# A two-layer graph network on one core: source tiles in pairs in layer 1, and where its memory and its small work lie

## The chip, the cores and the metric

The kernel runs on one core of a Trainium2 chip. The metric is the device time of one execution, in microseconds (us). A core has five engines that run side by side, each through its own queue of instructions in order: TensorE (PE; its weight loads are listed as PEld), VectorE (DVE), ScalarE (ACT), GpSimd (POOL) and SyncE (SP), which here only starts transfers. Engines wait for one another through semaphores.

## The reference, cut to what matters

Layer 0 is an attention with a random-walk branch, a normalisation, a residual and a second normalisation. Layer 1 is a graph attention with four heads, again with a residual and a normalisation. N is 2708 nodes, D is 256, H is 4 heads of 64.

```python
# layer 0
x = layernorm(x + layer0(x, adj))          # layer0 ends in layernorm(h) * ln_g + ln_b
# layer 1
Wh  = einsum('nd,hdo->nho', x, W)
s_i = einsum('nho,ho->nh', Wh, a_src); s_j = einsum('nho,ho->nh', Wh, a_dst)
e   = leaky_relu(s_i[:, None, :] + s_j[None, :, :], 0.2)
adj[i, i] = 1
att = softmax(where(adj != 0, e, -inf), axis=1)
x   = layernorm(x + einsum('ijh,jho->iho', att, Wh))
```

The kernel writes the exponential of the leaky ReLU as a product: up to factors that cancel in the softmax, exp(e) is max(r_i, t_j) times a factor s_j of the source. So `r` holds the targets' part, `tj` the sources', and `sb` the factor s_j. `v` is Wh already multiplied by s_j.

## The kernel before, in words

The nodes lie in 22 tiles: 16 of 128 rows and 6 of 110. `rows[t]` is the size of tile t and `off[t]` its first row.

**Layer 0** (`fast_layer0`) runs two steps of attention and walk. Its small stages are Python generators: `finish` adds the terms of a target tile, `norms` does its two layer normalisations, and `sources` makes `v`, `sb`, `tj` and `s_src` for layer 1 and stores `v` in device memory. A loop over slots advances them. For the last four tiles (`LATE`) `norms` and `sources` are left for layer 1. Memory comes from pools that lie one behind the other in the order in which they are opened: `heldp`, `finp`, `rowp`, `w0`, `keep` (with `xm`, `ba`, `rinv`, `qT`, `kT1`), `sortp`, `tpp`, `wk`. When layer 0 ends these are given up and the pools of layer 1 are opened from the same address. An instruction of layer 1 that writes there has to wait for the last user of what lay there before. `ba` is what the last attention (L258) reads, and `tpp` holds its turned weights `eT`.

**Layer 1** (`layer1`) goes over three groups of targets (8, 8 and 6 tiles: 1024, 1024 and 660 columns). Within a group it goes over all 22 source tiles; group 0 takes them in another order, `first`, with the late tiles last. `order` lists the 66 steps. For each step n:

- `mask(n)` loads a block of the transposed adjacency (and in group 0 the tile's `v`) through SP's queue and makes it 0 or 1 on ScalarE: Sign (L1193), then Square (L1198). If the source tile lies in the group, GpSimd sets its diagonal between the two (L1196, L1197).
- `weights(n)` computes four tiles `pt`, one for each head, on VectorE (L1272): the maximum of `r` and `tj`, times the mask. There are two sets of `pt`.
- `values(n)` multiplies them with `v` on TensorE (L1283), two heads side by side on 64 columns each; `denominators(n)` does the same with `sb` (L1293), four heads side by side on 32 columns each. Both add up over the 22 source tiles in six PSUM banks `acc`.

At a group's end `acc` is copied to `val` and `den`, and during the next group `settle` turns one target tile after another, divides, adds the residual, normalises and stores. Each normalisation takes the statistics on VectorE, adds the epsilon and takes the power -1/2 on GpSimd, and applies both on VectorE. The settles of the last group have nothing beside them and form the tail. In the middle of a group, `share` and `spread` bring `r` for the next group. `verdict` sums up whether the fast layer 0 was exact; it runs at once, in group 1.

Inside layer 1 the program order fixes what each of the four computing engines does. SP's queue is not in that list (`engines`), and its transfers are ordered by the planner. The loop before is:

```python
for n, (g, i, j) in enumerate(order):
    mask(n + 2)
    ...                      # late tiles, settles, share and spread
    weights(n + 1)
    values(n, (0, 1)); values(n, (2, 3))
    denominators(n)
```

Of the kernel before, what the change touches and what calls it, by code (L numbers as in the profile page):

```python
# [8 lines left out]
F32 = mybir.dt.float32  # L9
BF16 = mybir.dt.bfloat16  # L10
I32 = mybir.dt.int32
AF = mybir.ActivationFunctionType
# [32 lines left out]
def kernel(  # L45
# [61 lines left out]
    offdiag = const.tile([P, P], F32, name="offdiag")  # L107
    nc.vector.tensor_scalar(offdiag, ident, -1.0, 1.0, op0=ALU.mult, op1=ALU.add)
# [21 lines left out]
    def layernorm(dst, src, m):  # L130
# [6 lines left out]
        nc.gpsimd.tensor_scalar(ve[:m], mv[:m, 1:2], LN_EPS, None, op0=ALU.add)  # L137
        rs = small.tile([P, 1], F32, name="ln_rs")
        nc.gpsimd.tensor_tensor(rs[:m], ve[:m], minus_half[:m], op=ALU.pow)
        nc.vector.tensor_scalar(  # L140
# [3 lines left out]
    def sources(t, pool, room):  # L144
# [23 lines left out]
        nc.sync.dma_start(vd[t][:m], vt[:m])  # L168

    def norms(t, xt):  # L170

        m = rows[t]
        hh = xe[:m, t, 0:D]
        for last in range(2):
            st = small.tile([P, 6], F32, name="ln_st")[:m]
            mv = small.tile([P, 2], F32, name="ln_mv")[:m]
            nc.vector.bn_stats(st, hh)
            nc.vector.bn_aggr(mv, st)
            yield
            ve = small.tile([P, 1], F32, name="ln_ve")[:m]  # L180
            rs = small.tile([P, 1], F32, name="ln_rs")[:m]
            nc.gpsimd.tensor_scalar(ve, mv[:, 1:2], LN_EPS, None, op0=ALU.add)
            nc.gpsimd.tensor_tensor(rs, ve, minus_half[:m], op=ALU.pow)
            yield
            nc.vector.tensor_scalar(
                hh, hh, mv[:, 0:1], rs, op0=ALU.subtract, op1=ALU.mult
            )
            yield
            if not last:
                nc.gpsimd.tensor_mul(hh, hh, g_sb[:m])  # L190
                nc.gpsimd.tensor_add(hh, hh, b_sb[:m])
                nc.gpsimd.tensor_add(hh, hh, xt[:m])
                yield
# [73 lines left out]
    def general_layer0():  # L267
        with ExitStack() as l0:
# [199 lines left out]
            def finish(t, xf2, xa2):  # L468
# [23 lines left out]
                layernorm(hh[:m], hh[:m], m)  # L492
# [3 lines left out]
                layernorm(xt, hh[:m], m)  # L496
# [28 lines left out]
    def fast_layer0(ep, adjp):  # L525
# [3 lines left out]
        heldp, finp, rowp, w0, keep, sortp, tpp, wk = (  # L529
            l0.enter_context(tc.tile_pool(name=name, bufs=bufs))  # L530
            for name, bufs in (
                ("heldp", HELD), ("finp", 2), ("rowp", 2), ("w0", 1), ("keep", 1),
                ("sortp", 1), ("tpp", 3), ("wk", 1),
# [57 lines left out]
        ba = keep.tile([P, NT, D], F32, name="ba")  # L591
        rinv = keep.tile([P, NT], F32, name="rinv")
# [9 lines left out]
        kT = [wk.tile([P, HN], F32, name="junk"), keep.tile([P, HN], F32, name="kT1")]  # L602

# [357 lines left out]
        def finish(t, ac, ca, cb):  # L961
# [11 lines left out]
            nc.gpsimd.tensor_add(xt, xt, held.pop(t)[:m])  # L973
            if t < NT - LATE:
                yield
                yield from norms(t, ca)
                yield from sources(t, rowp, lambda: ps_tr.tile([P, 4, P], F32, name="tr"))
# [129 lines left out]
        def verdict(pt):  # L1107
# [4 lines left out]
            for s, r in enumerate(sorted_):  # L1112
# [6 lines left out]
                if s:  # L1119
                    nc.vector.tensor_tensor(wants, wants, haves, op=ALU.min)  # L1120
# [3 lines left out]
                    )  # L1124

# [6 lines left out]
                    )  # L1132

# [3 lines left out]
                else:  # L1137
# [3 lines left out]
                    )  # L1141
                nc.vector.scalar_tensor_tensor(
# [8 lines left out]
            )  # L1151
            nc.tensor.matmul(pt, total, ones, start=True, stop=True)
            nc.vector.tensor_scalar(
# [12 lines left out]
    def layer1(ep, adjp, r=None, verdict=None):  # L1166
        l1 = ExitStack()

        pp, rp, pj, keep = (
            l1.enter_context(tc.tile_pool(name=name, bufs=bufs))  # L1170
            for name, bufs in (("pp", 2), ("rp", 1), ("pj", 2), ("keep1", 1))
        )
        ps_u = l1.enter_context(tc.tile_pool(name="ps_u", bufs=2, space=PSUM))
# [6 lines left out]
        for t in reversed(first):  # L1180
            v[t] = keep.tile([P, H, FO], F32, name=f"v{t}")
# [4 lines left out]
        def neighbours(g, j):  # L1186
# [6 lines left out]
            nc.scalar.activation(bar, bar, AF.Sign)  # L1193
            if j in spans[g]:
                own = bar[:, off[j] - i0 : off[j + 1] - i0]
                nc.gpsimd.tensor_mul(own, own, offdiag[:k, :k])  # L1196
                nc.gpsimd.tensor_add(own, own, ident[:k, :k])  # L1197
            nc.scalar.activation(bar, bar, AF.Square)  # L1198
            return bar

        def settle(g, t, val, den, u, last):
# [12 lines left out]
            if last:  # L1214
# [3 lines left out]
            else:  # L1218
# [8 lines left out]
            st = small.tile([P, 6], F32, name="ln_st")[:m]  # L1227
            mv = small.tile([P, 2], F32, name="ln_mv")[:m]
            nc.vector.bn_stats(st, flat)
            nc.vector.bn_aggr(mv, st)  # L1230
            ve = small.tile([P, 1], F32, name="ln_ve")[:m]
            rs = small.tile([P, 1], F32, name="ln_rs")[:m]
            nc.gpsimd.tensor_scalar(ve, mv[:, 1:2], LN_EPS, None, op0=ALU.add)
            nc.gpsimd.tensor_tensor(rs, ve, minus_half[:m], op=ALU.pow)
            yield
            o = pp.tile([P, D], F32, name="o")[:m]
            nc.vector.tensor_scalar(
                o, flat, mv[:, 0:1], rs, op0=ALU.subtract, op1=ALU.mult
            )
            nc.sync.dma_start(out[off[t] : off[t + 1], :], o)  # L1240
# [24 lines left out]
        def weights(n):  # L1265
            if n < len(order):
                g, _, j = order[n]
                k, gw = rows[j], off[spans[g][-1] + 1] - off[spans[g][0]]
                probs[n] = [pj.tile([P, GW], F32, name=f"pt{h}") for h in range(H)]
# [30 lines left out]
        def prepared(t):  # L1300

            yield from norms(t, x_late[:, t - NT + LATE, :])
            yield from sources(t, pp, aux)


        late = [prepared(t) for t in range(NT - LATE, NT)] if verdict else []
        rest, running = [], []
        mask(0)
        mask(1)
# [116 lines left out]
```

## Time and profile before

| | |
|---|---|
| median of 3 runs | 1614.43 us (1613.76 to 1616.03) |
| the profiled execution | 1616.12 us, span from first to last instruction 1614.3 us |
| busy: TensorE, VectorE, ScalarE, GpSimd | 1555.1, 1225.7, 758.0, 475.0 us |
| layer 1, group 0 | 1230.6 to 1372.0 us |
| group 1 | 1372.0 to 1502.4 us |
| group 2 | 1502.4 to 1588.6 us |
| tail | 1588.6 to 1604.5 us, then the end of the program |

In the rows of the profile a tile is named without its number, `out<-in` says what is written and read, and the bracket behind a row gives the idle time before it and what ended it. A row of a timeline merges neighbouring instructions of one kind; "x16" is their number. A value or denominator matmul in this number format appears as two records, so one source tile has 16 records of each kind.

### The profile page before, as it was taken

How to read it: one execution, taken by the hardware profiler on the slowest of the kernel's cores; microseconds unless marked ns; L12 is line 12 of the kernel's file. 1: busy time of each engine (PE TensorE's matmuls, PEld its weight loads, DVE VectorE, ACT ScalarE, POOL GpSimd, SP SyncE). 2: the span in 40 equal slices, each digit the busy share in tenths (PEclk: the TensorE clock that was granted, in tenths of full speed). 3: DMA queues.
4: the chain of work that ended last, by engine and by line, in shares of the span. 5: the costliest groups of instructions: out<-in, count | busy, mean ns of one | idle time of the engine just before them, and what ended most of it. 6: DMA issues, size and time to landing. Idle time of an engine off the chain costs nothing.

```text
span 1614.3 us, 23771 instructions
## 1 busy us (share of the span) xinstructions
PE 1555.1 (96%) x8029; PEld 1032.9 (64%) x8029; DVE 1225.7 (76%) x3669; ACT 758.0 (47%) x1324; POOL 475.0 (29%) x908
## 2 busy tenths in 40 slices
PE   6999999999998999999999999999999989998994
PEld 3477777776776888787778888777785322222342
DVE  2777677677309767877878888989885969999995
ACT  2444444444345455555555665556633334443441
POOL 1311000001023122232124554555533820162143
PEclk9999999999999999999999999999999999999997
DMA  7200000000034333333333334343244242342331
GB/s 200 77 13 17 9 9 12 10 9 13 8 92 107 98 86 96 91 76 84 78 97 96 99 104 118 102 110 94 73 115 148 78 150 84 97 139 77 86 95 30
DMA packets 172493, 128.26 MB, mean 79 GB/s; under 512 B 44342, under 2 KB 161804, under 8 KB 172362
## 3 DMA queue, kind: packets, MB, share of 16 engines
q1 hardware_dynamic: 166442, 115.87, 26.5%
q0 software_dynamic: 3648, 9.26, 1.8%
q10 hardware_dynamic: 2272, 1.52, 0.3%
q8 instruction: 65, 1.06, 0.3%
q14 instruction: 66, 0.54, 0.1%
HBM read 111.78 MB, written 13.46 MB: 78 GB/s over the span
## 4 chain that ended last, share of the span: by engine, by line
PE 83%; DVE 9%; DMA 3%; POOL 2%; ACT 1%; issue 1%; SPq 0%; ACTq 0%; POOLq 0%; DVEq 0%
PE att L258 25%; PE walk L893 24%; PE acc L1283 8%; PE lg L658 7%; PE tr L240 6%; DVE pt L1272 5%; PE acc L1293 4%; PE tr L938 2%; PE tr L952 2%; DMA blk<-in_adjT_dram 2%; PE tr L155 1%; PE lg L628 1%; PE tr L628 1%; DMA xa<-in_w1T_dram 0%; POOL blk L1197 0%
## 5 line engine op out<-in xcount | busy, mean ns | idle before, releaser
L245 ACT COPY eT<-tr 128x512 f32<-128x512 f32 (+5 forms) x264 | 141.5, 537 | 289.2 <-PE tr L240 286.4
L683 ACT ACTIVATE junk<-e,minus,rth 128x2708 bf16<-128x2708 f32 (+1 forms) x88 | 232.8, 2646 | 19.5 <-POOL rth L715 18.6
L1283 PE MATMUL acc<-pt,v 128*64 128x512 f32 (+3 forms) x1056 | 227.9, 560 | 5.9 <-DVE pt L1272 3.7
L258 PE MATMUL att<-ba,eT 128*128 128x256 f32 (+3 forms) x968 | 230.8, 379 | 0.7 <-ACT eT L245 0.7
L258 PE MATMUL att<-xm,eT 128*128 128x256 f32 (+3 forms) x968 | 230.9, 380 | 0.4 <-ACT xa L1021 0.4
L893 PE MATMUL walk<-xe,blk 128*128 128x257 f32 (+3 forms) x968 | 225.3, 384 | 5.0 <-DVE xf L907 5.0
L893 PE MATMUL walk<-xm,blk 128*128 128x256 f32 (+3 forms) x968 | 222.1, 380 | 1.2 <-DVE xw L966 1.2
L893 PEld LDWEIGHTS walk<-xe,blk 128*128 128x128 f32 (+3 forms) x968 | 178.4, 186 | 50.3 <-issue 12.2
L1272 DVE SCALAR_TENSOR_TENSOR pt<-e,tj,blk 128x1024 f32<-128x1024 f32 (+3 forms) x176 | 190.1, 1142 | 25.0 <-PE att L258 9.4
L893 PEld LDWEIGHTS walk<-xm,blk 128*128 128x128 f32 (+3 forms) x968 | 177.6, 186 | 35.4 <-issue 4.2
L258 PEld LDWEIGHTS att<-ba,eT 128*128 128x128 f32 (+3 forms) x968 | 169.5, 186 | 22.4 <-ACT eT L245 1.2
L258 PEld LDWEIGHTS att<-xm,eT 128*128 128x128 f32 (+3 forms) x968 | 169.5, 186 | 22.1 <-ACT xa L1021 0.8
L662 ACT ACTIVATE e<-lg 128x1024 f32<-128x1024 f32 (+1 forms) x132 | 121.1, 922 | 115.0 <-PE lg L658 111.4
L1283 PEld LDWEIGHTS acc<-pt,v 128*64 128x64 f32 (+1 forms) x1056 | 74.4, 138 | 146.2 <-issue 108.2
L763 DVE MAX8 cand<-e 128x8 f32<-128x170 f32 (+1 forms) x352 | 89.6, 322 | 90.7 <-ACT e L662 90.6
L240 PEld LDWEIGHTS tr<-ident,e 128*128 128x128 f32 (+3 forms) x968 | 115.2, 138 | 55.7 <-issue 21.0
L240 PE MATMUL tr<-ident,e 128*128 128x128 f32 (+3 forms) x968 | 147.0, 271 | 0.3 <-ACT xe L944 0.3
L1193 ACT ACTIVATE blk<-blk 128x1024 f32<-128x1024 f32 (+3 forms) x66 | 63.2, 957 | 161.4 <-DMA blk<-in_adjT_dram 148.4
L1293 PE MATMUL acc<-pt,sb 128*32 128x512 f32 (+3 forms) x1056 | 113.6, 548 | 0.0
L1272 DVE SCALAR_TENSOR_TENSOR pt<-r,tj,blk 128x1024 f32<-128x1024 f32 (+1 forms) x88 | 111.1, 1324 | 3.2 <-PE acc L1293 2.1
L763 DVE MAX8 cand<-scr 128x8 f32<-128x97 f32 (+1 forms) x616 | 102.0, 244 | 0.0
L907 DVE TENSOR_TENSOR xf<-walk,xe 128x257 f32<-128x257 f32 (+1 forms) x22 | 9.4, 426 | 110.8 <-PE walk L893 110.8
(215 smaller groups left out, 1987.5 us busy)
## 6 DMA issues: line engine op xcount, KB each, us to landing
blk<-in_adjT_dram SPq DMA_DIRECT2D x32, 704.0 KB
blk<-in_adjT_dram SPq DMA_DIRECT2D x32, 512.0 KB
blk<-in_adjT_dram SPq DMA_DIRECT2D x48, 330.0 KB
blk<-in_adjT_dram SPq DMA_DIRECT2D x32, 320.0 KB
blk<-in_adjT_dram SPq DMA_DIRECT2D x12, 605.0 KB
blk<-in_adjT_dram SPq DMA_DIRECT2D x12, 440.0 KB
blk<-in_adjT_dram SPq DMA_DIRECT2D x18, 283.6 KB
c<-cs POOLq DMA_DIRECT2D x32, 128.0 KB, 2.0
```

The source lines that it names most:

```text
L240: nc.tensor.transpose(tr[: rows[t], q, :m], e[:m, off[t] : off[t + 1]], ident[:m, :m])
L245: copy(eT[:k, : len(grp), :m], tr[:k, : len(grp), :m])
L258: nc.tensor.matmul(acc, eT[: rows[t], q, :m], value(t), start=(t == 0), stop=(t == NT - 1),)
L658: nc.tensor.matmul(lg[:m, h, :w], qT[part, cols], kT[s][part, c0 : c0 + w], start=True, stop=True,)
L662: nc.scalar.activation(halves[:m, :, c0 : c0 + w], lg[:m, :, :w], AF.Exp, accum_out=zp[:m, n : n + 1],)
L683: nc.scalar.activation(junk[:m], e[:m], func, scale=rth, bias=minus1[:m], accum_out=acc)
L763: nc.vector.max(cand[:, n, :], src[:m, n * size : min(N, (n + 1) * size)])
L893: nc.tensor.matmul(ac[:m, :w], blk[: rows[j], j - j0, :m], cur[: rows[j], j, 0:w], start=(j == 0), stop=(j == NT - 1),)
L1193: nc.scalar.activation(bar, bar, AF.Sign)
L1272: nc.vector.scalar_tensor_tensor(pt[:k, :gw], targets[g][h // 2][:k, h % 2, :gw], tj[:k, j, h : h + 1], bar, op0=ALU.max, op1=ALU.mult,)
L1283: nc.tensor.matmul(acc[h // 2][c][q * FO : (q + 1) * FO, :w], v[j][:k, h, :], probs[n][h][:k, c0 : c0 + w], **at,)
L1293: nc.tensor.matmul(acc[2][c][h * 32 : (h + 1) * 32, :w], sb[:k, j, h : h + 1].to_broadcast([k, 32]), probs[n][h][:k, c0 : c0 + w], **at,)
```

## The change

1. **Pairs.** The loop of layer 1 goes over two source tiles at a time: the values of both, then the denominators of both. What stood at the head of each step is now the function `beside`, called before the first and after the denominators; only the first two of the late generators advance in a call.
2. **Other space.** There are three sets of `pt` (12 tiles, `DEEP = 3`) in place of two. Masks and weights are issued further ahead: three masks and two sets of weights before the loop. The pools of both layers are opened in another order: `ba` has a pool of its own behind `tpp` and `sortp`, and in layer 1 `pt` follows `pp` directly, then `v`, then `rp`. `v` lies in the order in which it is used. `val` and `den` have one buffer in place of two.
3. **Diagonals.** One maximum with the identity on VectorE, after Sign and Square, takes the place of two GpSimd operations between them. `offdiag` is gone.
4. **Norms.** All normalisations use `layernorm`, now a generator. The epsilon is added on VectorE, so GpSimd has one operation, the power. `b_sb` is added to `ca` in `finish` and no longer in `norms`.
5. **Queues and the rest.** The late tiles' `v` and the `out` of all groups but the last are stored from ScalarE's queue. `verdict` is a generator among the late ones. In the tail, even tiles are divided on ScalarE.

The diff, cut:

```diff
@@ layernorm, sources, norms @@
-        nc.gpsimd.tensor_scalar(ve[:m], mv[:m, 1:2], LN_EPS, None, op0=ALU.add)
+        nc.vector.tensor_scalar(ve[:m], mv[:m, 1:2], LN_EPS, None, op0=ALU.add)
         rs = small.tile([P, 1], F32, name="ln_rs")
         nc.gpsimd.tensor_tensor(rs[:m], ve[:m], minus_half[:m], op=ALU.pow)
+        yield
         nc.vector.tensor_scalar(
             dst, src, mv[:m, 0:1], rs[:m], op0=ALU.subtract, op1=ALU.mult
         )
-    def sources(t, pool, room):
+    def sources(t, pool, room, queue=nc.sync):
...
-        nc.sync.dma_start(vd[t][:m], vt[:m])
+        queue.dma_start(vd[t][:m], vt[:m])
...
+        yield from layernorm(hh, hh, m)
+        nc.gpsimd.tensor_mul(hh, hh, g_sb[:m])
+        nc.gpsimd.tensor_add(hh, hh, xt[:m])
+        yield
+        yield from layernorm(hh, hh, m)
+        yield
@@ fast_layer0 @@
-        heldp, finp, rowp, w0, keep, sortp, tpp, wk = (
+        heldp, finp, rowp, w0, keep, tpp, sortp, keepb, wk = (
...
-        ba = keep.tile([P, NT, D], F32, name="ba")
+        ba = keepb.tile([P, NT, D], F32, name="ba")
...
             nc.gpsimd.tensor_add(xt, xt, held.pop(t)[:m])
+            nc.gpsimd.tensor_add(ca[:m], ca[:m], b_sb[:m])
@@ layer1 @@
-            for name, bufs in (("pp", 2), ("rp", 1), ("pj", 2), ("keep1", 1))
+            for name, bufs in (("pp", 2), ("pj", 1), ("keep1", 1), ("rp", 1))
         )
+        DEEP = 3
...
-        for t in reversed(first):
+        for t in first:
             v[t] = keep.tile([P, H, FO], F32, name=f"v{t}")
...
             nc.scalar.activation(bar, bar, AF.Sign)
+            nc.scalar.activation(bar, bar, AF.Square)
             if j in spans[g]:
                 own = bar[:, off[j] - i0 : off[j + 1] - i0]
-                nc.gpsimd.tensor_mul(own, own, offdiag[:k, :k])
-                nc.gpsimd.tensor_add(own, own, ident[:k, :k])
-            nc.scalar.activation(bar, bar, AF.Square)
+                nc.vector.tensor_tensor(own, own, ident[:k, :k], op=ALU.max)
...
-            if last:
+            if last and t % 2:
...
+            yield from layernorm(o, flat, m)
+            if last:
+                nc.sync.dma_start(out[off[t] : off[t + 1], :], o)
+                return
+            yield
+            nc.scalar.dma_start(out[off[t] : off[t + 1], :], o)
...
-                probs[n] = [pj.tile([P, GW], F32, name=f"pt{h}") for h in range(H)]
+                probs[n] = [pj.tile([P, GW], F32, name=f"pt{h}_{n % DEEP}") for h in range(H)]
...
+        if verdict:
+            late.append(verdict(aux))
+        def beside(g, i):
+            for part in late[:2]:
...
+        for n in range(DEEP):
+            mask(n)
+        for n in range(DEEP - 1):
+            weights(n)
+
+        for n in range(0, len(order), 2):
+            g, i, j = order[n]
+            beside(g, i)
+            weights(n + 2)
+            mask(n + 3)
...
+            for u in (n, n + 1):
+                for k in range(2):
+                    values(u, (2 * k, 2 * k + 1))
...
+            for u in (n, n + 1):
+                denominators(u)
...
+            else:
+                beside(g, i + 1)
+            weights(n + 3)
+            mask(n + 4)
```

## The prediction

> **What bounds the kernel now.** I read the page's busy table first, then the table by stretches for the three target groups of layer 1, then TensorE's and VectorE's timelines inside them, the waits, and last the chain at both ends of the layer. The edits outside layer 1 are small, so layer 1 (1230.6 to 1604.5 us) is the place.
>
> ```profile
> 1230.60:1372.00 141.40, 133.67 (x729) 38.94 (x729) 124.15 (x117) 51.58 (x80) 58.53 (x45) 0.98 0.38 117
> 1372.00:1502.40 130.40, 125.95 (x735) 35.58 (x731) 122.53 (x146) 53.57 (x81) 41.65 (x40) 0.97 0.36 102
> 1502.40:1588.60 86.20, 86.20 (x733) 36.09 (x729) 82.64 (x119) 37.47 (x75) 30.33 (x36) 1.00 0.30 82
> ```
>
> Columns: stretch, length, busy time of TensorE, its weight loads, VectorE, ScalarE and GpSimd, clock, DMA. Groups 0, 1 and 2 take 141.4, 130.4 and 86.2 us. TensorE looks fuller, but VectorE is busy for 124, 123 and 83 of them: two engines near their limits.
>
> ```profile
> 1339.38 3.65 PE L1283 MATMUL acc<-pt,v 128*64 128x512 f32 x16
> 1342.96 1.92 PE L1293 MATMUL acc<-pt,sb 128*32 128x512 f32 x16
> 1344.82 3.65 PE L1283 MATMUL acc<-pt,v 128*64 128x512 f32 x16
> ...
> 1502.43 2.44 PE L1283 MATMUL acc<-pt,v 128*64 128x512 f32 x16
> 1504.80 1.32 PE L1293 MATMUL acc<-pt,sb 128*32 128x512 f32 x16
> 1506.05 2.44 PE L1283 MATMUL acc<-pt,v 128*64 128x512 f32 x16
> ```
>
> Undisturbed, a source tile costs TensorE 5.44 us (3.58 values, 1.86 denominators), in group 2 3.62. The single records start 0.429 us apart in the values and 0.430 in the denominators: 8 x 0.429 = 3.43 and 4 x 0.430 = 1.72. The remaining 0.15 + 0.14 = 0.29 us is lost at the two changes of kind; in group 2 it is the same 0.29.
>
> ```profile
> 1222.48 0.72 POOL L972 TENSOR_TENSOR xe<-xe,xw 110x256 f32<-110x256 f32 x1 [5.72 <-ACT xw L968]
> 1230.60 4.47 SPq L1260 DMA_DIRECT2D v<-v  x10
> 1230.62 5.33 DVE L1272 SCALAR_TENSOR_TENSOR pt<-e,tj,blk 128x1024 f32<-128x1024 f32 x4 [9.41 <-PE att L258]
> 1232.78 6.18 PE L1283 MATMUL acc<-pt,v 128*64 128x512 f32 x16 [2.25 <-DMA v<-v]
> ```
>
> The head: VectorE stands 9.4 us until the last attention frees the memory under `pt`; then TensorE waits for the first weights and `v`, and its first values take 6.18 instead of 3.65.
>
> ```profile
> 1241.74 4.85 DVE L1272 SCALAR_TENSOR_TENSOR pt<-e,tj,blk 128x1024 f32<-128x1024 f32 x4
> 1247.39 5.68 DVE L1272 SCALAR_TENSOR_TENSOR pt<-e,tj,blk 128x1024 f32<-128x1024 f32 x4
> 1247.71 1.50 POOL L191 TENSOR_TENSOR xe<-xe,b_sb 110x256 f32<-110x256 f32 x1
> ...
> 1329.52 6.67 DVE L1272 SCALAR_TENSOR_TENSOR pt<-e,tj,blk 128x1024 f32<-128x1024 f32 x5 [6.74 <-ACT blk L1198]
> ...
> 1478.42 0.19 PE L1152 MATMUL aux<-ones,total 128*1 128x1 f32 x2 [4.45 <-DVE total L1149]
> ...
> ACT blk L1198 <- POOL blk L1197: 43.3, 22, 6.2
> ```
>
> VectorE needs 4.79 us for four weights (starts 1.196 apart; the row adds the last one's drain), 5.6 with GpSimd beside it. Its one long stall, 6.74, follows the broadcast of `r`, which delays the mask loads. The verdict stops TensorE for 4.45. The diagonals hold ScalarE 22 times, 43 us, mostly in its slack.
>
> **The change part by part.**
>
> *Pairs.* Two tiles share one change to denominators and one back: 0.29 / 2 = 0.143 us less per tile: 5.294 and 3.474. TensorE's own work: group 0, 22 x 5.294 + 6 for the late sources (four times 1.14 + 0.35) = 122.5; group 1, 116.5 + 8 settles x 0.48 + 0.4 = 120.7; group 2, 76.4 + 3.8 = 80.2.
>
> *Other space, three `pt` sets.* By the sizes in the code, the first two sets of `pt` now lie over `rowp`, `w0` and `xm`. The last users of those are L966, L968 and L972, which ends at 1223.2. So VectorE can start 7.4 us earlier and prepare almost two tiles; the first two `v` lie over `kT1`, long free, so TensorE starts at 1230.6. The other `v` still wait for the attention. If the loads of masks stand behind them on SP, up to 5 us (the row of ten `v`) is lost: rival two. If they don't, nothing; I take nothing.
>
> *Diagonals on VectorE.* Two GpSimd operations leave the path between Sign and Square, 22 VectorE maxima of 128x128 come. No row has that form: below, a 128x22 operation took 0.18; above, 128x154 took 0.315. I take 0.25: 2, 2 and 1.4 us in the groups. A gain here is excluded on VectorE[...]. They now stand in VectorE's queue behind the weights of the tile before and wait there for ScalarE's Square; the next weights and GpSimd's norms are behind them. A load took 4.9 us (1235.98 to 1240.86) and two passes 2.1; two tiles of weights give 9.6. The cover is 2.6 us.
>
> *Norms.* The epsilon addition moves to VectorE: 0.19 each (small dependent operations start 0.15 to 0.19 apart). 8 late norms and 16 settles before the tail, so 1.5 us per group. In layer 0, 36 x 0.19 = 6.8 us more VectorE lie under a TensorE that is 100% busy from 1000 to 1180 while VectorE has 156 of 180; I take 0, and 2 if the search becomes late. `b_sb` moves within GpSimd, sum 0. A norm is then 0.55 (statistics) + 0.19 + 0.33 = 1.07, a settle 1.2 with its reciprocal.
>
> *Queues.* 4 stores of `v` and 16 of `out` go from SP to ScalarE's queue: 20 issues x 0.35 = 7 us, on an engine with 52 of 141 busy. Each waits for its producer, with Sign and Square behind it; the added yield puts the producer half a pair earlier, so 0. SP loses the stops before L168.
>
> *One `val` and `den` instead of two.* The copies at a group's end now wait for the transposes of the group before. Those ended at 1463 and 1564, the copies came at 1500 and 1586: 0. They stand in VectorE's queue between two tiles' weights and wait for the pair's denominators; a copy took 0.7, and I count 0.8 for the waiting in each of two groups. `offdiag` was one operation at the start: 0.
>
> *Verdict.* Its 28 operations, 5 us, go to group 0's second half, and TensorE no longer waits: 4.45 + 2.1 (values of 5.79 instead of 3.65) leave group 1.
>
> [...] The rows: in 1339.3 to 1366.6 TensorE keeps 5.44 per tile and VectorE idles 0.56 before each tile. [...] By the rows TensorE sets these tiles now[...]. I count both loads.
>
> GpSimd's L190 to L192 beside the weights cost VectorE 0.4 per operation (weights 1.58 apart instead of 1.196). [...] 24 remain (8 late, 16 settles): 9.6 by the row[...]. I use the row.
>
> **The sum.** VectorE in group 0, first six pairs: 57.5 weights + 8.6 norms + 3.2 GpSimd + 0.5 + 1.5 waits for GpSimd (a row of 1.5) = 71.3, so 1223.2 to 1294.5. Last five: 47.9 + 1.5 + 5 + the stall of 6.7 = 61.1: 1355.6. TensorE trails by its last value half and the pair's denominators, 1.7 + 3.6: 1361 (its own work of 122.5 from 1230.6 would end at 1353). Before, 1372.0: gain 11. Group 1: eight pairs with settles 9.57 + 1.2 + 0.4 + 0.2 = 11.35 (TensorE 11.07), three at TensorE's 10.59, 1.9 for copies and share: 124.5 instead of 130.4, gain 5.9. Group 2: a pair with settle took VectorE 7.80, now 7.97: 8 x 8.0 + 3 x 6.95 = 85.0 instead of 86.2, gain 1.2. Tail: six chained norms of 2.27, 0.1 less each, one slower ScalarE result: 0.3. Together 18.4. The profiled execution took 1616.1 (span 1614.3, 1.8 around it): 1597.7. It lies 1.7 above the median of the runs, so the forecast is **1596.0**.
>
> **The rivals.** *TensorE stays the bound:* VectorE's stalls vanish too, and 122.5 + 120.7 + 80.2 from 1230.6 ends at 1554, 34.6 earlier: 1579.5. For it: less GpSimd. Against: group 2's VectorE is 96% busy. 0.10.
>
> *The head gains nothing:* `pt` still waits for the attention (7.4 lost, 1603.4), or also the masks behind `v` (4 more, 1607.4). For it: SP's ten `v` in one block at 1230.60. This is also the case that the other space doesn't do what it should. 0.20.
>
> *Slower:* the diagonals make VectorE wait for ScalarE as ScalarE now waits for GpSimd. Each of 22 then costs d more; it decides at d = (18.4 + 3.2) / 22 = 0.98. With 1.2, 26.4 - 18.4: 1622. For it: loads after the broadcast took 7.6. Against: the cover of 2.6. 0.05.
>
> **How the numbers follow.** My case has 0.65 and its own range 1588 to 1604 (loads 4, diagonals 2[...], stalls 6 the other way). 1586 to 1609 takes in most of the second rival and leaves out the first, the slower one and some edge. 0.2% (3.2 us) is about what can be told from no change. Faster 0.93; same 0.03, from the edges of rivals two and three; slower 0.04.
>
> **What would show it.** Right: the first weights near 1223, 32 value records then 32 denominators, about 10.6 us per quiet pair; VectorE over 95% in groups 1 and 2, and TensorE waiting for `pt`. Wrong: a first weight near 1230, a VectorE wait on L1193/L1198 at each diagonal, group 2 clearly under 83 or over 88 us, or a layer 0 that ends elsewhere.

## The result and the profile after

The changed kernel takes 1599.5 us (median of 4 runs, 1598.88 to 1600.24) and the kernel before 1614.22 (4 runs beside it, 1613.76 to 1616.03). The ratio is 0.9906, with a 95% interval of 0.9894 to 0.9918, so the gain is 14.7 us where 18.4 were forecast. The profiled execution of after took 1599.23 us, with a span of 1597.4.

The page's busy table, and the table by stretches for the three groups of layer 1 (length, then TensorE, its weight loads, VectorE, ScalarE, GpSimd, clock, DMA):

```profile
PE 1542.9 (97%) x8029; PEld 1039.1 (65%) x8029; DVE 1226.0 (77%) x3753; ACT 760.4 (48%) x1336; POOL 393.0 (25%) x798
...
1236.17:1364.01 127.84, 125.72 (x732) 39.82 (x732) 117.92 (x148) 50.65 (x79) 17.67 (x17) 0.99 0.43 125
1364.01:1485.08 121.07, 121.07 (x734) 38.09 (x730) 119.30 (x139) 53.11 (x81) 22.62 (x16) 1.00 0.39 108
1485.08:1571.78 86.70, 86.70 (x733) 38.91 (x729) 82.88 (x133) 37.33 (x75) 17.29 (x16) 1.00 0.30 81
```

GpSimd does 82 us less over the whole program. In group 1 TensorE is busy for all of its 121.07 us (before 125.95 of 130.40). VectorE is busy for 98.5% of group 1 and 96% of group 2.

The head of layer 1, in the timeline of after:

```profile
1226.65 10.12 DVE L1258 SCALAR_TENSOR_TENSOR pt<-e,tj,blk 128x1024 f32<-128x1024 f32 x8 [1.72 <-POOL xe L957]
...
1233.59 2.22 SPq L1246 DMA_DIRECT2D v<-v  x5
...
1236.17 7.09 PE L1269 MATMUL acc<-pt,v 128*64 128x512 f32 x32 [2.66 <-DMA v<-v]
...
1243.19 3.64 PE L1279 MATMUL acc<-pt,sb 128*32 128x512 f32 x32
1246.76 7.09 PE L1269 MATMUL acc<-pt,v 128*64 128x512 f32 x32
```

VectorE no longer waits for the attention but for GpSimd's addition at L957, and eight weights come without a stop, 6.9 us before the attention ends. The matmuls come 32 and 32: 10.59 us for a quiet pair (1236.17 to 1246.76). But every `v` was still loaded after the attention (1233.59), and TensorE waited 2.66 us for it.

Laid against one another by the records' times (the end of the last L243/L258, the first value of each group, the last denominator, the last instruction):

| stretch, us | before | after | difference | forecast |
|---|---|---|---|---|
| to the end of the last attention | 1230.53 | 1233.51 | +3.0 | 0 |
| from there to group 1's first value | 141.48 | 130.50 | -11.0 | -11 |
| group 1 | 130.42 | 121.07 | -9.3 | -5.9 |
| group 2, to its last denominators | 86.23 | 86.77 | +0.5 | -1.2 |
| tail | 25.55 | 25.54 | 0.0 | -0.3 |
| sum | 1614.2 | 1597.4 | -16.8 | -18.4 |

The sum is that of the profiled executions. Before's lay 1.9 above its median and after's 0.3 below, hence 14.7 between the medians. The forecast came close partly by luck, by way of a loss and a gain that it did not have: layer 0 became longer, and group 1 shorter than thought. The -11.0 of group 0 is in part luck too (see the first point on why the prediction was right).

**Where layer 0 lost 3 us.** The timeline of after around a late source tile, in layer 0:

```profile
1177.78 3.03 DVE L817 SCALAR_TENSOR_TENSOR e<-scr,fact,e 110x2708 f32<-110x2708 f32 x1
...
1177.94 3.27 POOL L137 TENSOR_TENSOR ln_rs<-ln_ve,minus_half 110x1 f32<-110x1 f32 x1 [6.71 <-DVE ln_ve L135]
...
1183.43 3.47 DVE L733 SCALAR_TENSOR_TENSOR scr<-e,hi 110x2708 f32<-110x2708 f32 x1
...
1187.61 0.41 DVE L139 TENSOR_SCALAR xe<-xe,ln_mv,ln_rs 110x256 f32<-110x256 f32 x1
...
1188.16 0.38 PE L148 MATMUL tr<-ident,xe 110*128 110x110 f32 x2 [2.61 <-DVE xe L139]
```

The last step of a normalisation (L139) stands in VectorE's queue behind the search's large operations, and TensorE, which has the turning of that row (L148) next in its queue, stands for 2.61 us. In before TensorE has no stop above 0.6 us between 913 us and the end of the attention. It is not the epsilon's addition that does this: with it back on GpSimd (experiment 4) the stand is the same,

```profile
1187.38 0.38 PE L148 MATMUL tr<-ident,xe 110*128 110x110 f32 x2 [2.49 <-DVE xe L139]
```

What is left of the change there is the order: before, a normalisation stopped between statistics, power and application; now statistics, epsilon and power come in one turn, so that L139 falls elsewhere among the search's operations. Laid side by side matmul by matmul, after is 2.0 us behind before ahead of this stand, 3.7 behind it, and 3.0 at the attention's end. Experiment 6, which has no such stand, is 2.0 behind at the same place and 0.5 at the end. Where the first 2.0 come from stays open.

**Half-speed windows.** A second thing that the forecast lacked shows in the clock column. TensorE had stretches of 3.41 us in which its clock read 0.50. After, around 1295.6, then before, around 1233.7, by stretches:

```profile
1292.20:1295.60 3.40, 1.82 (x14) 0.60 (x8) 3.40 (x6) 2.35 (x4) 0.00 (x0) 1.00 0.23 29
1295.60:1299.01 3.41, 3.41 (x10) 0.98 (x8) 3.41 (x4) 1.56 (x2) 0.00 (x0) 0.50 0.32 127
1299.01:1302.40 3.39, 3.39 (x18) 1.15 (x16) 3.29 (x5) 0.56 (x1) 0.00 (x0) 1.00 0.51 153
```

```profile
1233.71:1237.12 3.41, 3.41 (x11) 1.12 (x12) 3.38 (x5) 0.00 (x0) 0.52 (x1) 0.50 0.77 225
1237.12:1240.53 3.41, 3.41 (x24) 0.80 (x20) 3.41 (x4) 0.00 (x0) 2.10 (x2) 1.00 0.92 290
```

The waits ahead of the window in after, and what it does to the next 32 values (7.09 us elsewhere):

```profile
1294.51 0.71 PE L148 MATMUL aux<-ident,xe 110*128 110x110 f32 x4 [1.58 <-DVE xe L139]
1295.15 8.78 PE L1269 MATMUL acc<-pt,v 128*64 128x512 f32 x32
```

A window cost 1.7 us where TensorE had work throughout: these values took 8.78 instead of 7.09, 1.69 more, and in experiment 6 8.74, 1.65 more. Before had four of them in layer 1 (1233.7, 1332.7 and two on end at 1476.1), after has one; the tail, where TensorE has little to do, is left out (20.8 us at half clock there in before, 20.6 in after). TensorE stood for part of the pair at 1476.1 (4.45 us, up to 1478.42), and the sixteen values behind that took 5.79 instead of 3.65, so by an estimate from these lengths the windows lost 1.7 + 1.7 + 2.2 = 5.6 us before and 1.7 after. Up to about 3.9 of the 16.8 us are therefore windows that did not come. Of the sixteen values that took 6.18 us, a window makes 1.7 of the 2.5 us above the usual 3.65, and the 5.79 us, which the prediction counted with a wait, are such a window.

Layer 0 had windows as well. Of the eight kernels in which TensorE stands at L148, six (experiments 1, 2, 3, 4, 5 and 7) have one right behind that stand, at 1187.2 to 1189.4; after and experiment 12 have none. In experiment 1:

```profile
1187.89 0.38 PE L148 MATMUL tr<-ident,xe 110*128 110x110 f32 x2 [2.60 <-DVE xe L139]
...
1189.43:1192.84 3.41, 3.41 (x12) 2.57 (x11) 2.10 (x13) 0.79 (x2) 0.00 (x0) 0.50 0.73 160
```

Against before, TensorE falls back by 1.7 us there in after and in experiment 12, and by 3.2 to 3.6 in these six. All kernels but experiments 3 and 7 also have one near 517. In the comparisons below the number of windows is given where it matters; it is known for the profiled executions alone, while the medians come from all.

### The profile page after: what moved, and what is told of

Same layout as the page of the kernel before. It is cut to its first block, busy times and chain, and to the rows that moved or that the text cites. A ratio compares the mean times of both kernels' runs of the same rounds, so it can differ in the third digit from the quotient of the medians.

```text
span 1597.4 us, 23674 instructions
## 1 busy us (share of the span) xinstructions
PE 1542.9 (97%) x8029; PEld 1039.1 (65%) x8029; DVE 1226.0 (77%) x3753; ACT 760.4 (48%) x1336; POOL 393.0 (25%) x798
## 4 chain that ended last, share of the span: by engine, by line
PE 90%; DVE 6%; ACT 1%; issue 1%; POOL 1%; DMA 1%; ACTq 0%; POOLq 0%; DVEq 0%; SPq 0%
PE att L243 25%; PE walk L878 24%; PE acc L1269 13%; PE lg L643 7%; PE tr L225 6%; PE acc L1279 6%; PE tr L923 2%; PE tr L937 2%; DVE pt L1258 1%; PE tr L154 1%; PE lg L613 1%; DVE scr L814 1%; DVE scr L733 1%; PE tr L613 1%; DVE e L817 1%
## 5 line engine op out<-in xcount | busy, mean ns | idle before, releaser
L243 PE MATMUL att<-xm,eT 128*128 128x256 f32 (+3 forms) x968 | 230.9, 380 | 0.4 <-ACT xa L1007 0.4
L243 PE MATMUL att<-ba,eT 128*128 128x256 f32 (+3 forms) x968 | 230.7, 379 | 0.2 <-ACT eT L230 0.2
L1269 PE MATMUL acc<-pt,v 128*64 128x512 f32 (+3 forms) x1056 | 218.0, 549 | 2.9 <-DMA v<-v 2.7
L1258 DVE SCALAR_TENSOR_TENSOR pt<-e,tj,blk 128x1024 f32<-128x1024 f32 (+3 forms) x176 | 186.2, 1122 | 6.2 <-PE acc L1279 2.5
L243 PEld LDWEIGHTS att<-xm,eT 128*128 128x128 f32 (+3 forms) x968 | 169.6, 186 | 22.1 <-ACT xa L1007 0.8
L243 PEld LDWEIGHTS att<-ba,eT 128*128 128x128 f32 (+3 forms) x968 | 169.5, 186 | 21.7 <-ACT eT L230 0.5
L137 POOL TENSOR_TENSOR ln_rs<-ln_ve,minus_half 128x1 f32<-128x1 f32 (+1 forms) x66 | 66.3, 1004 | 224.7 <-DVE ln_ve L135 174.6
L1279 PE MATMUL acc<-pt,sb 128*32 128x512 f32 (+3 forms) x1056 | 106.8, 545 | 0.0
```

Source lines behind the costliest of these rows:

```text
L243: nc.tensor.matmul(acc, eT[: rows[t], q, :m], value(t), start=(t == 0), stop=(t == NT - 1),)
L1258: nc.vector.scalar_tensor_tensor(pt[:k, :gw], targets[g][h // 2][:k, h % 2, :gw], tj[:k, j, h : h + 1], bar, op0=ALU.max, op1=ALU.mult,)
L1269: nc.tensor.matmul(acc[h // 2][c][q * FO : (q + 1) * FO, :w], v[j][:k, h, :], probs[n][h][:k, c0 : c0 + w], **at,)
L1279: nc.tensor.matmul(acc[2][c][h * 32 : (h + 1) * 32, :w], sb[:k, j, h : h + 1].to_broadcast([k, 32]), probs[n][h][:k, c0 : c0 + w], **at,)
```

## The experiments

The first four are the kernel after with one thing undone or moved, the next three remove one cost each, 8 to 11 combine these, and 12 varies the first. Times are medians, each with its ratio to the kernel before that was measured beside it; "after" without more is 1599.5. Those medians of before lie between 1613.96 and 1615.50, so a difference of 1 us between medians of two experiments shows little, and the parts are read from the stages. Stage lengths are from the profiles, by the same records as above.

**1. The pairs alone undone.**

```diff
             for u in (n, n + 1):
                 for k in range(2):
                     values(u, (2 * k, 2 * k + 1))
...
-            for u in (n, n + 1):
-                denominators(u)
+                denominators(u)
```

> The changed kernel, but each tile's denominators follow its own values again (values, denominators, values, denominators); all else stays. The changed kernel took 1599.5. Theory A (TensorE sets groups 0 and 1, VectorE sets group 2): each tile costs TensorE 0.143 us more, so 22 x 0.143 = 3.1 more in group 1, 2 to 3 in group 0, 0 to 1 in group 2: 1604 to 1606. Rival B (VectorE is the bound in all groups after the change): the pairing is covered, 1599 to 1600.5, and group 1 stays at 121.

Measured 1603.39 (0.9924, 0.9908 to 0.9941), 3.9 more than after and a little under theory A's range. By stretches, groups 1 and 2, then TensorE's timeline of one pair with a settle, here and in after:

```profile
1368.37:1491.87 123.50, 123.50 (x734) 34.97 (x730) 119.38 (x139) 53.21 (x81) 22.60 (x16) 1.00 0.38 104
1491.87:1577.43 85.56, 85.56 (x732) 36.30 (x728) 82.94 (x133) 37.20 (x75) 17.27 (x16) 1.00 0.31 81
```

```profile
1391.08 3.65 PE L1269 MATMUL acc<-pt,v 128*64 128x512 f32 x16
1394.66 1.92 PE L1279 MATMUL acc<-pt,sb 128*32 128x512 f32 x16
1396.51 3.65 PE L1269 MATMUL acc<-pt,v 128*64 128x512 f32 x16
...
1402.43 3.65 PE L1269 MATMUL acc<-pt,v 128*64 128x512 f32 x16
```

```profile
1386.65 7.09 PE L1269 MATMUL acc<-pt,v 128*64 128x512 f32 x32
1393.66 3.64 PE L1279 MATMUL acc<-pt,sb 128*32 128x512 f32 x32
...
1397.71 7.09 PE L1269 MATMUL acc<-pt,v 128*64 128x512 f32 x32
```

Group 1 is 2.4 us longer than in after: a pair with a settle takes TensorE 11.35 instead of 11.07, a quiet one 10.88 instead of 10.59, the 0.28 of the forecast, and 11 times that is 3.1. About 0.7 of it is given back: 0.5 at the group's start, where the paired kernel's first pair takes 11.57 while the copies of the group before are made, and 0.2 in its last two pairs. Group 0, from TensorE's start, is 3.0 longer, of which one more window makes 1.7, and layer 0 is 1.8 longer, which its window explains. Group 2, which VectorE sets, is 1.1 *shorter* without pairs: behind the last weights come, in pairs, the denominators of two tiles (a row of 2.43 us) and not of one. With the windows taken off, pairing is worth about 2.5 us in all, less than the 3.9 between the medians.

**2. The early start alone undone:** `ba` goes back into the pool `keep`, so the memory under `pt` is again held by the last attention.

```diff
-            ba = keepb.tile([P, NT, D], F32, name="ba")
+            ba = keep.tile([P, NT, D], F32, name="ba")
```

> The changed kernel, but `ba` lies in the pool `keep` again, so that the pool of `pt` lies over memory that the last attention still reads. Both theories: the first weights start at about 1233.6 instead of 1226.6. Theory A (the early start counts): TensorE's first pair waits for the second tile's weights and group 0 has less lead: 3 to 5 us, 1602.5 to 1604.5. Rival B (TensorE waits for the first `v` until 1236.2 anyway, and group 0 has slack): below 1 us, 1599.5 to 1600.5.

Measured 1608.92 (0.9960, 0.9946 to 0.9974), 9.4 more than after and well above both expectations. VectorE's timeline:

```profile
1234.45 10.59 DVE L1258 SCALAR_TENSOR_TENSOR pt<-e,tj,blk 128x1024 f32<-128x1024 f32 x8 [8.67 <-PE att L243]
```

The first weight comes 7.8 us later than in after and group 1 starts 10.0 later (0.8 of it from a longer layer 0, which has a window; group 0 has one window in both); groups 1 and 2 are the same to 0.01 us. TensorE began within 0.4 us of after, so it is VectorE's start that sets the end of group 0, and almost all of the delay stays. This is the largest single part of the gain.

**3. No diagonals** (the maximum at L1191 is left out, and so are the ones on the diagonal of the mask).

> The changed kernel without the 22 maxima on the diagonal; the diagonals are left as the adjacency has them. It measures what the diagonals on VectorE cost on the path. Theory A (TensorE sets groups 0 and 1): only group 2 gains, six of 0.2: 1 to 1.5 us, 1598 to 1598.5. Rival B (VectorE sets all groups): 22 x 0.2 = 4.4 us, 1595. Rival C (the maxima make VectorE wait for ScalarE's Square): more than 5 us, with the waits on L1188 gone.

Measured 1596.62 (0.9881, 0.9864 to 0.9897), 2.9 less; the profile has one window fewer than after in the whole program, which is 1.7. Group 0 is 1.4 shorter, less than the window of after that this kernel does not have, so nothing is shown there; group 1 0.2, group 2 1.07 for 6 diagonals. The row takes 0.28 us, and the next instruction starts 0.20 after it began (forecast 0.25). In after, VectorE's waits at L1191 are two, nearly all in one of them, where ScalarE had stood for TensorE's projection of a late source tile (L154) with the mask's passes behind it:

```profile
DVE blk L1191 <- ACT blk L1188: 3.5, 2, 3.3
...
1308.61 0.17 ACT L158 ACTIVATE sb<-aux 110x4 f32<-110x4 f32 x1 [9.04 <-PE aux L154]
...
1313.95 0.29 DVE L1191 TENSOR_TENSOR blk<-blk,ident 128x128 f32<-128x128 f32 x1 [3.28 <-ACT blk L1188]
```

That is 3.5 us in all, or 0.16 for each of 22 diagonals, where the third rival needed 0.98; and without the diagonals VectorE still stops for 2.60 us at this point, for the same passes. No run puts the diagonals back on GpSimd, so what moving them gained is not shown, only what they cost on VectorE.

**4. The epsilon on GpSimd again, in all norms.**

```diff
-        nc.vector.tensor_scalar(ve[:m], mv[:m, 1:2], LN_EPS, None, op0=ALU.add)
+        nc.gpsimd.tensor_scalar(ve[:m], mv[:m, 1:2], LN_EPS, None, op0=ALU.add)
```

> The changed kernel with the epsilon of every normalisation added on GpSimd again, two dependent GpSimd operations as before. Theory A (VectorE sets group 2): VectorE is relieved of 8 x 0.15 there, about 1 us gained, 1598 to 1599. Rival D (GpSimd's second small operation is blocked behind the weights, so the results come late and VectorE or TensorE waits for them): 1601 or more, with waits on the power in groups 0 to 2. The 2.6 us that TensorE waits in layer 0 for a normalised row may change with either.

Measured 1594.91 (0.9874, 0.9858 to 0.9891), 4.6 less, a larger gain than theory A's: this part of the change cost time. Group 2 is 1.7 shorter (85.07), which is 8 times 0.21; group 1 0.2; group 0 1.2, no more than the missing window; that window stands in layer 0 instead, which is 0.9 longer, so the two profiles have equally many. The tail is 1.6 shorter, though its last `o` comes 0.8 *later* after the denominators (16.4 against 15.6): between the last `o` and the end of the program lie 7.6 us instead of 10.0. All four kernels with the epsilon on GpSimd have this shorter tail (23.9 to 24.0 us), and its cause stays open, all the more since before, with the same norm, has 9.7 behind the last `o`. Rival D did not come: the two GpSimd operations took 1.18 and 1.46 us beside the weights in before (1241.91 and 1243.17) and 0.22 and 0.57 in the tail here, and no stage of layer 1 became longer by it.

**5. The first two `v` in a pool of their own**, ahead of the others.

```diff
-            v[t] = keep.tile([P, H, FO], F32, name=f"v{t}")
+            v[t] = (early if t in first[:2] else keep).tile([P, H, FO], F32, name=f"v{t}")
```

> The changed kernel, but the first two `v` have a pool of their own between `pt` and the other `v`, at the same addresses. Theory E (an instruction waits for everything that lay under its whole pool, so one pool for all `v` made the first ones wait for the last attention): these two loads start near 1226 instead of 1233.6, TensorE's wait of 2.66 us goes: 1597 (1596.5 to 1597.5). Rival F (the order of SP's queue held them, or TensorE then waits for the second or third weights instead): below 0.7 us, 1599 to 1599.8.

Measured 1600.07 (0.9913, 0.9896 to 0.9930): no gain, and the windows are as many as in after (here in layer 0). The timeline, SP's queue and TensorE:

```profile
1227.63 0.80 SPq L1246 DMA_DIRECT2D v<-v  x2
...
1236.36 7.09 PE L1269 MATMUL acc<-pt,v 128*64 128x512 f32 x32 [0.56 <-ACT xa L1007]
```

Two loads now start 6.0 us before those of after and 8.2 before the attention ends, and TensorE's wait falls from 2.66 to 0.56. So the memory of the first two `v` was free, as the prediction had it, but they were allotted from a pool whose other tiles lay over the attention's memory, and the wait was for the pool. From VectorE's first weight to group 1 it took 135.8 us, as in after without its window (137.4 less 1.7). TensorE's start was not what counted.

**6. One more turn for other work before the normalised source rows** in layer 0, so that VectorE finishes L139 before TensorE comes to L148.

```diff
                 yield from norms(t, ca)
+                yield
```

> The changed kernel with one more yield in layer 0 between the second normalisation and the turning of the row on TensorE. Theory G (the 2.6 us that layer 0 lost are TensorE standing at L148 behind a normalised row that VectorE's search holds back): the wait goes, the last attention ends 2.6 us earlier: 1597 (1596.5 to 1597.5). Rival H (the additional VectorE work of 6.8 us makes the search itself late): the attention ends as now, 1599 to 1600.

Measured 1598.74 (0.9904, 0.9888 to 0.9921). TensorE's timeline:

```profile
1189.68 0.35 PE L148 MATMUL tr<-ident,xe 110*128 110x110 f32 x2
...
1233.19 8.74 PE L1270 MATMUL acc<-pt,v 128*64 128x512 f32 x32 [2.13 <-DMA v<-v]
```

The wait is gone, and the attention ends at 1231.06 instead of 1233.51. Yet the time is within 0.8 us of after: a window more than in after fell on the first values (8.74 instead of 7.09, 1.65 us). From the attention's end group 0 is 1.9 longer, so that 0.3 is left without a cause that I found. Alone this run shows the mechanism and not its worth; runs 8, 9 and 11 do that.

**7. The settles' normalisation applied by ScalarE** (in groups 0 and 1, so during groups 1 and 2). A small GpSimd operation forms the bias.

```diff
+                nc.gpsimd.tensor_scalar(
+                    mr[:m], mv[:m, 0:1], rs[:m], -1.0, op0=ALU.mult, op1=ALU.mult
+                )
...
+                nc.scalar.activation(o, flat, AF.Identity, scale=rs[:m], bias=mr[:m])
```

> The changed kernel, but in the settles before the tail the normalisation is applied on ScalarE, with the product of mean and root made by one more small GpSimd operation. VectorE loses 16 operations of 0.32. Theory A (VectorE sets group 2, TensorE the others): 8 x 0.32 = 2.6 less in group 2, nothing in group 1: 1597 (1596.5 to 1598). Rival B (VectorE sets all groups): 5 us, 1594.5. Rival I (the result now waits on ScalarE behind the masks): 0 or slower.

Measured 1597.46 (0.9894, 0.9877 to 0.9910), 2.0 less. By stretches, groups 1 and 2:

```profile
1365.31:1486.15 120.84, 120.84 (x734) 37.50 (x730) 115.67 (x131) 57.69 (x89) 41.48 (x24) 1.00 0.39 109
1486.15:1570.45 84.30, 84.30 (x733) 38.45 (x729) 80.15 (x125) 41.88 (x83) 29.68 (x24) 1.00 0.31 82
```

VectorE has 3.6 us less to do in group 1, and group 1 does not move (120.84); it has 2.7 less in group 2, and that becomes 2.4 us shorter. So TensorE sets group 1 and VectorE group 2.

**8. Edits 5, 6 and 7 together.**

> The three last edits together: the first two `v` in their own pool, the later turn in layer 0, the normalisation applied on ScalarE. If they are independent, 2.6 + 2.6 + 2.5 less than 1599.5: 1592. If one takes the cover of another (for instance an earlier start that group 0's VectorE can't use), 1594 to 1596.

Measured 1591.90 (0.9865, 0.9849 to 0.9882), 7.6 less than after: alone they gave -0.6, 0.8 and 2.0, which sums to 2.2. Windows make a part of the other 5.4: by the profiles 6 has one more than after, 5 and 7 as many, and this kernel one fewer. At 1.7 each that leaves about 2 without a cause shown. Its profile is 8.5 shorter than that of after: 2.3 in layer 0 (the attention ends at 1231.18), 3.1 in group 0 (TensorE starts at 1231.75; 1.7 is the window), 0.2 in group 1, 2.4 in group 2 and 0.4 in the tail. VectorE's first weight to group 1 takes 134.3 us (135.7 in after without its window).

**9. As 8, and the epsilon on GpSimd.**

> The three edits tried together before (the first two v in a pool of their own, one more turn for other work before the normalised source rows of a target tile, the settles' normalisation applied by ScalarE; 1591.9 us) and the epsilon addition of every norm on GpSimd instead of VectorE. Theory: a 0.2 us VectorE operation per settle costs time where VectorE sets the end, and only there. Group 0 (126.85) and group 2 (84.36) then get shorter by about 1 us each (8 x 0.19 is the ceiling of each, 1.5), group 1 stays at TensorE's 120.8, and the time is 1588.5 to 1590.5. Rival: with the application gone to ScalarE, VectorE no longer sets the end and GpSimd's chain of two small operations per norm does; then nothing is gained, 1591.5 to 1593.

Measured 1587.60 (0.9829, 0.9812 to 0.9845), the fastest kernel here, 11.9 below after and 27.5 below the before measured beside it. By stretches, groups 1 and 2:

```profile
1358.46:1479.30 120.84, 120.84 (x734) 37.46 (x730) 114.11 (x123) 57.72 (x89) 42.76 (x32) 1.00 0.38 109
1479.30:1562.34 83.04, 83.04 (x733) 37.66 (x729) 79.08 (x117) 41.77 (x83) 33.42 (x32) 1.00 0.31 84
```

Group 2 is 1.3 shorter than in 8 and group 1 the same, as expected; group 0 is 0.5 longer and not 1 shorter, counted from a start 0.6 earlier. The tail gives 1.2, as in 4, and brings the time below the 1588.5 to 1590.5 expected.

**10. As 9, with group 2 unpaired.**

> As the kernel with all four edits, but in group 2 the denominators of each tile follow its own values (no pairs there). Theory: group 2 is set by VectorE, and with single tiles TensorE starts its next work half a pair earlier after each pair of weights, which in the unpaired kernel made this group 1.1 us shorter (85.64 against 86.77); here the same 0.5 to 1.1 us less in group 2, groups 0 and 1 unchanged. Rival: VectorE has been relieved so far that TensorE's own work counts; then 11 more changes of kind at 0.29 us make group 2 up to 3 us longer (83.3 is TensorE's own unpaired work, 80.2 paired).

Measured 1588.91 (0.9838, 0.9822 to 0.9854). Group 2 takes 83.48 instead of 83.10 us. Neither figure came: the 1.1 us that single tiles gave in group 2 in experiment 1 are gone, and the loss is 0.4. TensorE's own unpaired work, 80.2 and 22 times 0.143, is 83.3 and fits that, as VectorE has less to do than in experiment 1 (79.15 of these us). The ratios' intervals overlap, so the two medians cannot be told apart for certain.

**11. After with only 4 and 6.**

> The kernel after with only two edits: the epsilon addition on GpSimd in every norm, and one more turn for other work before the normalised source rows in layer 0. If the two gains add up, layer 0 ends about 2 to 3 us earlier (attention at 1231 instead of 1233.5) and groups 0 and 2 keep the gains of the epsilon edit alone (1594.91): 1592 to 1594. If they are one and the same, because the epsilon edit's gain in layer 0 is already the extra turn's, the time is 1594.5 to 1595.5.

Measured 1592.65 (0.9867, 0.9851 to 0.9884; 1590.15 to 1594.71), 6.9 below after with two lines changed, and 2.3 below experiment 4. The attention ends at 1230.93 against 1234.41 in 4, where 1.7 is the window behind the stand. In the profiles, the five kernels with the extra turn (6, 8, 9, 10, 11) end it at 1230.6 to 1231.2, after and the seven others at 1233.5 to 1235.8.

**12. Two sets of `pt`, unpaired.** This is experiment 1 with the weights of tile n + 2 issued behind the denominators of tile n.

```diff
-                probs[n] = [pj.tile([P, GW], F32, name=f"pt{h}_{n % DEEP}") for h in range(H)]
+                probs[n] = [pj.tile([P, GW], F32, name=f"pt{h}_{n % 2}") for h in range(H)]
...
-            weights(n + 2)
-            mask(n + 3)
...
+                denominators(u)
+                if u == n:
+                    weights(n + 2)
+                    mask(n + 3)
```

> As the unpaired kernel (1603.39; group 1 123.50, group 2 85.64 us), with two sets of pt instead of three: the weights of tile n + 2 are issued behind the denominators of tile n. Theory: the forecast of group 1 was too long because the third set lets VectorE work ahead in pairs without a settle and spend that lead in pairs with one; with two sets each slow pair of VectorE stops TensorE, and group 1 becomes 1 to 3 us longer (124.5 to 126.5), its TensorE no longer busy without a gap. Rival: VectorE's slow pairs are simply shorter than I costed them, and the third set is only what the pairs need; then group 1 stays at 123.5 (within 0.4).

Measured 1608.14 (0.9955, 0.9938 to 0.9971), 4.75 more than experiment 1. By stretches, groups 1 and 2:

```profile
1371.80:1495.31 123.51, 123.51 (x734) 34.98 (x731) 120.36 (x141) 53.34 (x81) 22.31 (x16) 1.00 0.39 107
1495.31:1581.75 86.44, 86.44 (x733) 37.01 (x729) 83.14 (x133) 36.99 (x75) 17.24 (x16) 1.00 0.31 83
```

Group 1 takes 123.50 as with three sets: the rival's figure, and my forecast of a longer group 1 fell. The third set is worth its time elsewhere, in group 0 (136.03 against 130.81, of which windows make about 1.7) and 0.9 us in group 2. The rival's reason, slow pairs that are shorter than costed, does not hold either, since VectorE's pairs with a settle are *longer* (next section). The unpaired TensorE takes 11.35 us for such a pair, so there is hardly a lead to spend; the run was a poor test of what the third set does in pairs. Pairs with two sets weren't tried.

## Why the prediction was right, and where it was not

- **Early start and group 0: right.** It said 1223.2 for VectorE's first weight, with TensorE's start 7.4 us later; the weight came at 1226.65, 6.9 before the end of the attention. From there to group 1 it took 137.4 us, a half-speed window among them, where 137.8 (1361 less 1223.2) were forecast. That this agrees to 0.4 us is luck: without the window it is 135.7, and the three terms of the sum were 73.1, 57.1 and 7.1 us (VectorE's first six pairs, its last five, TensorE's trailing) where 71.3, 61.1 and 5.3 stood. The last five were shorter mainly because the stall of 6.7 us behind the broadcast of `r` did not come again: VectorE's only long stop there is the 3.28 us of experiment 3, ahead of the broadcast (1315.44). Experiment 2 takes the early start away and loses 9.4. The second rival (the head gains nothing) is excluded by it.
- **`v` over `kT1`: the step failed, its cost did not.** "TensorE starts at 1230.6" took the addresses of tiles for what counts; the pool's memory came as one. TensorE started 2.66 us after the attention. Experiment 5 shows both the wait and that it cost nothing, as VectorE set group 0.
- **Layer 0: a term put at nothing.** The prediction took 0 for the norms in layer 0, since VectorE idles 24 of 180 us there, and "2 if the search becomes late". It weighed the 6.8 us of additions and not the order. What came late was a norm behind the search's operations, and TensorE behind that: 3.0 us, and the stand is there with the additions on GpSimd as well (experiment 4). The mean idle of an engine said nothing of the one instruction that another waits for. The five kernels with one more turn show it.
- **Pairs: right in kind, a little large.** 3.1 us in group 1 by the rows, 2.4 by experiment 1. In group 2 they cost 1.1, where no cost was forecast.
- **Verdict: right.** TensorE does not stop for it any more:

```profile
1342.71 0.19 PE L1144 MATMUL aux<-ones,total 128*1 128x1 f32 x2
```

The 4.45 of that wait left group 1. The 2.1 counted with it ("values of 5.79 instead of 3.65") were right in size but were a half-speed window that followed the wait.
- **Group 1: mis-sized by 3.4.** The sum made the eight pairs with a settle run at VectorE's 11.35 and the rest at TensorE's 10.59. VectorE's timeline in after, the first weights of pairs:

```profile
1379.19 10.28 DVE L1258 SCALAR_TENSOR_TENSOR pt<-r,tj,blk 128x1024 f32<-128x1024 f32 x8
...
1390.22 5.22 DVE L1258 SCALAR_TENSOR_TENSOR pt<-r,tj,blk 128x1024 f32<-128x1024 f32 x4
...
1401.50 5.22 DVE L1258 SCALAR_TENSOR_TENSOR pt<-r,tj,blk 128x1024 f32<-128x1024 f32 x4
...
1412.98 5.33 DVE L1258 SCALAR_TENSOR_TENSOR pt<-r,tj,blk 128x1024 f32<-128x1024 f32 x4
...
1469.61 4.87 DVE L1258 SCALAR_TENSOR_TENSOR pt<-r,tj,blk 110x1024 f32<-110x1024 f32 x4
...
1479.51 3.35 DVE L1258 SCALAR_TENSOR_TENSOR pt<-e,tj,blk 128x660 f32<-128x660 f32 x4
```

The eight slow pairs lie between 1379.19 and 1469.61: 90.4 us, and 8 x 11.35 is 90.8. So VectorE's cost was right, and single pairs take up to 11.6. TensorE needs 8 x 11.07 = 88.6 for its eight. But VectorE does its last pair in 9.90 (1469.61 to 1479.51), where TensorE takes 10.6, and starts group 2 5.6 us before TensorE does: the 1.9 us that it is slower in eight pairs it makes good in the others, and TensorE never stops. Taking the longer of the two engines pair by pair and adding up overstates a stage in which one can run ahead: by 8 x 0.28 = 2.2 of the 3.4 us. The other 1.2 are in the 1.9 us for copies and share, which cost TensorE 0.7. The lead is read from these rows; experiment 12, meant to show it, did not.
- **Group 2: 1.8 too short.** 86.77 where 85.0 were forecast. VectorE's pairs with a settle take 8.05 to 8.43 instead of 8.0 (but the first, 7.81), and the forecast left out that TensorE trails VectorE by the last values and two tiles' denominators, which it had counted in group 0. Experiments 3, 4 and 7 shorten the group by 1.07, 1.7 and 2.4, about what they take from VectorE, so VectorE sets it, as forecast.
- **Epsilon on VectorE:** 1.5 us per group was right for group 2 (1.7), and nearly nothing for group 1 (0.2), where TensorE sets the end. In group 0 no run separates it from the windows.
- **Diagonals: right.** 0.20 instead of 0.25 each, and the third rival's wait, of a diagonal for ScalarE, came once at length (3.28), at a point where VectorE stops without the diagonals too (2.60), and not at each diagonal. The first rival (TensorE as the bound, 1579.5) fell in groups 0 and 2; in group 1 TensorE did become the bound, and its 120.7 us for that group is nearer to the 121.07 measured than my 124.5.
- **Not tested.** No run undoes the stores from ScalarE's queue, the single `val` and `den` or the tail's division on ScalarE; that they cost nothing is in keeping with the sums and not shown.
- **Which engine sets group 1, and GpSimd beside VectorE.** By the prediction's rows TensorE set the tiles of group 1 before. Experiments 1 and 7 answer for the kernel after: 3.6 us less on VectorE changed 0.2 there, and 22 changes of kind on TensorE changed 2.4. So the row (TensorE full in each tile) held. GpSimd's power, 0.55 us in the median of after, took 3.27 beside VectorE's 3.03 in the rows of layer 0 above; in the settles the row's 0.4 for VectorE stayed (5.22 and 5.33 for four weights with GpSimd beside them, 4.86 without).

## What to carry to other kernels

When two engines are nearly full, ask of each stage which one ends it and how far the other can run ahead: time taken from the engine that does not end the stage was worth next to nothing here (3.6 us less on VectorE gave 0.2 in group 1), and an operation of 0.2 us put on the one that does was paid each time (eight made 1.7 us in group 2). A small step that moves in a queue has to be followed to the instruction that waits for it, since the mean idle time of its engine does not show that it stands behind an operation of 3 us (3.03 and 3.47 in the rows of layer 0). And a forecast summed from parts can be close while its parts are off, so check the parts by stage. Count a buffer as free only when the whole pool from which it comes is (with a pool of their own, the first two `v` cost TensorE 0.56 us of waiting instead of 2.66).

## What the runs showed of the hardware that was not expected

TensorE's clock read 0.50 for stretches of 3.413 us. One came behind an idle time of 1.58 us (after, 1292.9) and one behind 2.25 us (before's first values), and none came behind others as long: after's 2.66 us at 1233.5 has none behind it, and experiment 2 has 1.58 us idle at 1302.7 without one. In before the starts at 1233.71, 1332.70 and 1476.06 lie 98.99 and 143.36 us apart, which are 29 and 42 times 3.413. In after, the 3.40 us ahead of the stretch at 1295.6 held 1.82 us of TensorE's work; the 3.40 us from 1233.50 held 0.74, and the clock stayed at 1.00 behind them. So the length of an idle time did not tell here whether such a stretch came, and what decides it was not shown. At 1.7 us each, one more or one fewer is larger than several of the parts measured here, and so stage lengths were compared with the windows counted.
